# Moving two expert loads, seven weighted sums and two split positions in a Mamba and mixture-of-experts kernel

## The chip, the cores and the metric

The kernel runs on one core of one Trainium2 chip. The metric is the device time of one execution in microseconds (us); lower is better. A core has a matrix engine (PE, with its weight loads listed as PEld), a vector engine (DVE), an activation engine (ACT), GpSimd (POOL) and a sync engine (SP), which here issues all the DMAs. Each engine works through its own list of instructions in order, and an instruction that has to wait holds up everything behind it on the same engine.

## The reference

The input is 4 sequences of 1024 tokens with 128 features. Three layers are added to it in turn: a mixture of 8 experts (half weight), a Mamba layer, and the same mixture of experts again.

```python
x = x + 0.5 * _L0_ffn_ref(_layernorm(x, axis=-1), ...)
x = x + _L0_attn_ref(_layernorm(x, axis=-1), ...)
x = x + 0.5 * _L0_ffn_ref(_layernorm(x, axis=-1), ...)
```

The mixture computes every expert for every token and adds them with a weight per token:

```python
router_probs = softmax(x @ w_router)
gate_weights = softmax(x @ w_gating / GATE_TEMP)
h = silu(x @ w_gate[e]) * (x @ w_up[e])        # 128 -> 512, for each of 8 experts
expert_out = h @ w_down[e]                     # 512 -> 128
cw = router_probs * gate_weights
cw = cw / (sum(cw) + 1e-09)
out = sum over e of expert_out[e] * cw[:, e]
```

The Mamba layer projects to 2 x 256 channels, applies a causal convolution of 4 taps and Silu, derives the step `dt` (softplus) and the vectors B and C, and runs the recurrence `h = exp(dt * A) * h + dt * x * B` over 16 states per channel. Its output `sum(h * C) + D * x` is gated with Silu(z) and projected back. Everything is float32.

## The kernel before

**Tiling.** The 4096 tokens are cut into 8 blocks of 512 (`TB`), and a block lies transposed, 128 features by 512 tokens. Each block passes the mixture twice, so there are 16 mixture passes `s`; `order` lists them as (layer, block), beginning (1,0), (1,1). A pass goes through 8 experts. The text calls `s * E + e` a *position*: positions 0 to 7 are the first pass, 8 to 15 the second. The 512 hidden units of an expert are 4 chunks of 128, which are handled as 2 chunk pairs.

**One chunk pair.** `gate_part` makes the gate products in PSUM (`pg`, through `half_products`, lines 641 to 643) and takes Silu of them on ACT (`h`, line 625). `up_part` makes the up products (`pu`, the same lines) and multiplies them into `h` on DVE (line 657). `down` accumulates the expert's output in `pd`. Gate and up products are made of three fast matmuls: activations and weights are split into a rounded high part and a low part (`xh`, `xl`, `wh`, `wl`). The weights of an expert are split once, by two DVE instructions (`split_expert`, lines 298 and 299), from a raw buffer `wraw` into which `load_expert` brings them. Experts 0, 3 and 6 share one such buffer (tag `xc`), the others have two (tag `y`). `load_expert` issues three DMAs: gate and up weights to `wraw`, down weights to `wd`.

**Split positions.** For the positions in `SPL` the down product is made of three fast matmuls as well. That needs a split of the down weights (`wds`: ACT line 610, DVE line 612) and, for each chunk pair, `hh` on ACT (line 665) and `hl` on DVE (line 667); PE then runs the matmuls of lines 697 and 705, half an expert later than the ones it replaces. At other positions PE runs the plain float32 product of line 722.

**The weighted sum.** When an expert's `pd` is complete, ACT copies it to SBUF (`take`, line 735). Then `weight` multiplies it by the mixing weight `cwb` (line 744) and, except for the first expert, adds it to `acc` (line 747). Where `own` is true these are DVE instructions, else POOL's, in `pool_put`. `own` holds for positions 0 to 8 (`OWN = 9`) and for the whole last pass.

**The mixing weights.** `cwt` (line 556) transposes a pass's mixing weights, ACT copies them to `ct`, four small DMAs store them in DRAM (line 563), and `load_cw` reads them back spread over the 128 partitions (`cwb`, three buffers, line 588). In the first pass `cwt` stands at slot 11 (`CWT0`).

**Order.** All instructions are written out in an order that Python decides while it builds the kernel. Time is counted in *slots*, four for a chunk pair, 8 for a position, 64 for a pass. Each chain of events has slots at which its events are due; an event can also have a condition, and is forced when it is a number of slots late. `Plan` holds an estimated clock for each engine and puts the waiting pieces of DVE work (`put`, `fill`) and ACT work (`act_put`, `act_fill`) where they fit. `plan.need` writes out DVE work until a condition holds. Nothing in the order depends on times on the chip. Expert `e` is loaded at slot `8 * (e - 1) + WL`, with `WL = -5`, and its split is put at `8 * (e - 1) + WS`, `WS = 1`:

```python
    for e in range(1, E):
        add(8 * (e - 1), [(WL, lambda e=e: load_expert(e)), (WS, lambda e=e: split_expert(e))])
```

The Mamba layer of the first block starts around slot 77. Its scan (DVE lines 1015, 1021, 1033; ACT exponentials line 1002) starts when its softplus is done and goes on, block after block, until near the end.

Of the kernel before, what the change touches and what calls it, by code (L numbers as in the profile page):

```python
# [37 lines left out]
POW = 4  # L38
WL = -5
WS = 1  # L40
SPL = (*range(1, 11), *range(113, 127))
OWN = 9
CWT0 = 11
FENDS = {0: 8, 1: 9, 9: 9, 15: 8}
# [9 lines left out]
class Plan:  # L54
# [69 lines left out]
    def put(self, fn, cost, ready=0.0, low=False):  # L124
        it = [fn, cost, max(ready, 0.0), False]
        (self.lo if low else self.hi).append(it)
        return it
# [45 lines left out]
def tile_macaron_mamba_moe(  # L173
# [23 lines left out]
    E, _, F = w_gate.shape  # L197
# [20 lines left out]
    plan = Plan()  # L218
# [4 lines left out]
    def misc(name):  # L223
        if plan.reader in plan.spare:
            plan.act_need(plan.reader)
        plan.need(lambda: plan.reader is None or plan.reader[3])
        plan.wait_bank(name)
        return ps.tile([P, TB], F32, tag="misc", bufs=1, name=name)

    assert NBLK == 8  # L230
    order = [(1, 0), (1, 1), (1, 2), (1, 3), (2, 0), (1, 4), (2, 1), (1, 5), (2, 2), (1, 6), (1, 7)]
# [20 lines left out]
    def load_router():  # L252
        nc.sync.dma_start(out=wrg[:, 0:E], in_=w_router)
        nc.sync.dma_start(out=wrg[:, E:NE2], in_=w_gating)
# [19 lines left out]
    wh, wl, wd, raws, cast = {}, {}, {}, {}, {}  # L274

    def load_expert(e):
        tag, bufs = (("xc", 1), ("y", 2))[e % 3 > 0]
        raw = sb.tile([P, 2, F], F32, tag=tag, bufs=bufs, name=f"wraw_{e}")
        nc.sync.dma_start(out=raw[:, 0, :], in_=w_gate[e])
        nc.sync.dma_start(out=raw[:, 1, :], in_=w_up[e])  # L280
        if e == 0:
            load_router()
        wd[e] = const.tile([P, FC * H], F32, name=f"wd_{e}")
        nc.sync.dma_start(
            out=wd[e].rearrange("p (c h) -> p c h", c=FC),
            in_=w_down[e].rearrange("(c p) h -> p c h", p=P),
        )
        wh[e] = const.tile([P, 2, F], F32R, name=f"wh_{e}")
        wl[e] = const.tile([P, 2, F], F32R, name=f"wl_{e}")
        raws[e] = raw  # L290
# [5 lines left out]
    def split_expert(e):  # L296
        raw = raws.pop(e)
        plan.put(lambda: V.tensor_copy(wh[e], raw), 0.69, plan.pe)  # L298
        cast[e] = plan.put(lambda: V.tensor_tensor(wl[e], raw, wh[e].bitcast(F32), ALU.subtract), 1.21, plan.pe)  # L299
# [284 lines left out]
    def load_cw(s, e):  # L584
        d = ffn[s]
        kind, k = order[s]
        t = sb.tile([P, TB], F32, tag="cwb", bufs=3, name=f"cwb_{kind}_{k}_{e}")
        nc.sync.dma_start(out=t, in_=d["cd"][e, :].partition_broadcast(P))
        d["cwb", e] = t
        d["cwb_at", e] = max(plan.pe, d["cd_at"]) + 2.6  # L590

    def split(s, e):
        return s * E + e in SPL

    def gate_part(s, c):
# [7 lines left out]
        nm = f"{kind}_{k}_{c}"  # L603
        if f == 2 and s * E + e + 1 in SPL:
            x = (e + 1) % E
# [70 lines left out]
    def down(s, c):  # L676
        d = ffn[s]
        kind, k = order[s]
        e, f = divmod(c, FC)
        if f == 0:  # L680
            for o in list(ffn.values()):
                if "take" in o:
                    plan.act_need(o["take"])
            d["pd"] = ps.tile([P, TB], F32, tag="pd", bufs=1, name=f"pd_{kind}_{k}_{e}")
            if (s, e) == (len(order) - 1, E - 1):
                d["pds"] = d["pd"], misc("pd_end")
        h = d.pop(("h", c))
        cols = slice(f * H, (f + 1) * H)
        if len(h) == 2:
            ws = wds[s * E + e]  # L690
            w = ws["w"]
            if f % 2 == 0:
                plan.act_need(ws["wh"], d["hh", c])
                plan.need(lambda: ws["wl"][3])
                for q in range(2):
                    for i in range(2):
                        T.matmul(  # L697
                            d["pd"], w[:, i, (f + q) * H : (f + q + 1) * H], h[0][:, q, :],
                            start=(f + q + i == 0), stop=False,
                        )  # L700
                t = plan.on_pe(0.92, max(d["hh", c][4], ws["wl"][4]))
            else:
                plan.need(lambda: d["hl", c][3])
                for q in range(2):
                    T.matmul(  # L705
                        d["pd"], w[:, 0, (f + q - 1) * H : (f + q) * H], h[1][:, q, :],
                        start=False, stop=(f == FC - 1 and q == 1),
                    )
                t = plan.on_pe(0.46, d["hl", c][4])
        elif (s, e) == (len(order) - 1, E - 1):  # L710
            d["rest"] = d.get("rest", ()) + h
            if f % 2:
                for q in range(2):
                    part = slice(q * TB // 2, (q + 1) * TB // 2)
                    for g in (f - 1, f):
                        T.matmul(
                            d["pds"][q][:, 0 : TB // 2], wd[e][:, g * H : (g + 1) * H], d["rest"][g][:, part],
                            start=(g == 0), stop=(g == FC - 1),
                        )
            t = plan.on_pe(0.86, d["h_at", c])  # L720
        else:
            T.matmul(d["pd"], wd[e][:, cols], h[0], start=(f == 0), stop=(f == FC - 1))  # L722
            t = plan.on_pe(0.86, d["h_at", c])
        if f < FC - 1:
            return
        pd = d["pd"]
        edge = (s, e) == (len(order) - 1, E - 1)
        own = s * E + e < OWN or s == len(order) - 1

        def take():  # L730
            if e == 0:
                t = d["acc"] = sb.tile([P, TB], F32, tag="acc", bufs=2, name=f"acc_{kind}_{k}")
            else:
                t = sb.tile([P, TB], F32, tag="tmp", bufs=TMP, name=f"tmp_{kind}_{k}_{e}")
            S.copy(t, pd)

            def weight():
                cwb = d.pop(("cwb", e))
                at = max(plan.act, d["cwb_at", e])
                if e + 2 < E:  # L740
                    load_cw(s, e + 2)
                G_ = V if own else G
                put = (lambda f, cost, at: plan.put(f, 0.66, at)) if own else pool_put
                it = put(lambda: G_.tensor_tensor(t, t, cwb, ALU.mult), 1.25, at)  # L744
                if e > 0:
                    acc = d["acc"]
                    it = put(lambda: G_.tensor_tensor(acc, acc, t, ALU.add), 1.25, at)  # L747
                d["sum"] = it
                if e == E - 1:
                    d["tail"] = True  # L750
                    pool_run(None)

            if ("cwb", e) in d:
                weight()
            else:
                d.setdefault("late", []).append(weight)

        if edge:
            finish(d, d["pds"], k)
        else:  # L760
            d["take"] = plan.act_put(take, 0.58, t, True)
# [74 lines left out]
    def pool_run(after):  # L836
        credit[0] = min(credit[0] + CAP, CAP)
        while pend and (after is None or credit[0] > 0.0):
            pool_one(after)
# [309 lines left out]
    def add(base, evs, wait=WAIT):  # L1149
        chains.append([(max(0, base + ev[0]), wait, *ev[1:]) for ev in evs])  # L1150
# [13 lines left out]

    GPS = E
    add(0, [(0, lambda: load_expert(0))])
    for s in range(len(order)):
        add(8 * GPS * s, ffn_events(s))
# [8 lines left out]
        add(START[k], mid, 99)  # L1177
        add(START[k], back, 40)
    for e in range(1, E):
        add(8 * (e - 1), [(WL, lambda e=e: load_expert(e)), (WS, lambda e=e: split_expert(e))])  # L1180
    add(8 * E, [(-24, load_mamba)])

    S.preload_act_table_set("silu_and_others")
# [3 lines left out]
    with tc.manual_schedule(engines={ET.PE, ET.Activation, ET.DVE, ET.Pool, ET.SP}):  # L1187
        half = 0
        while chains or done < nst:
            c = 2 * half  # L1190
            todo = []
            while done < min(nst, c - 2 * (done // FC in SPL)):
                todo.append(done)
# [47 lines left out]
```

## Time and profile before

| | |
|---|---|
| time, 3 runs | 1262.14 us median (1262.1 to 1264.05) |
| the profiled execution | 1264.02 us, of which its span of instructions 1262.2 us |
| busy PE | 1245.7 us, 99% of the span |
| busy DVE | 1141.8 us, 90% |
| busy ACT | 920.8 us, 73% |
| busy POOL | 705.8 us, 56% |
| DMA | 115.09 MB, mean 91 GB/s |
| plain down product, line 722 | 824 instructions, two for each matmul call |
| Silu(g) * u, DVE line 657 | 256 instructions, 1214 ns |
| weighted sum on POOL, lines 744 and 747 | 98 pairs, 1348 and 1329 ns |

Busy time is the sum of the instructions' durations without overlaps; matmuls are pipelined, so a busy PE is not PE at its peak. The time around the span (1.8 us in the profiled execution) belongs to the launch and does not depend on the instructions. The span cut in 40 slices of 31.6 us, busy share in tenths (9 is 90% or more):

```profile
PE   9999999999999999999999999999999999999998
DVE  5986599999999999999999999999999999998676
ACT  6676887776778678877788787767876867656653
POOL 1012465767557656874576568656866575564400
PEclk9999999999999999999999999999999999999999
```

### The profile page before, as it was taken

Reading aid. Unit: us, or ns where it says so; the run is one execution under the profiler, and the core shown is the slowest. Engines: PE = TensorE matmul, PEld = TensorE weight load, DVE = VectorE, ACT = ScalarE, POOL = GpSimd, SP = SyncE. Lnnn points to the kernel's source line nnn. Section 1 sums busy time; section 2 is a strip of 40 time slices with the busy share of each in tenths; the row PEclk is TensorE's granted clock in tenths of the full one; section 3 lists DMA queues with packets and bytes.
Section 4 is the critical chain, followed back from the end, with each engine's and each line's share of the span. In section 5 each row is a group of like instructions: output and inputs, shape, how many; then the busy total and the mean of one; then the engine's idle time right before and its main releaser. Section 6 shows DMA issues by size and latency. Waiting matters only on the chain. (4 is left out here: it accounts for less than half of the span.)

```text
span 1262.2 us, 14418 instructions
## 1 busy us (share of the span) xinstructions
PE 1245.7 (99%) x4800; PEld 861.0 (68%) x4800; DVE 1141.8 (90%) x1286; ACT 920.8 (73%) x1324; POOL 705.8 (56%) x557
## 2 busy tenths in 40 slices
PE   9999999999999999999999999999999999999998
PEld 6777666666666666666666666666666666667887
DVE  5986599999999999999999999999999999998676
ACT  6676887776778678877788787767876867656653
POOL 1012465767557656874576568656866575564400
PEclk9999999999999999999999999999999999999999
DMA  4501333243333433333433343433433433311110
GB/s 135 171 24 36 103 109 90 88 127 86 96 95 92 120 89 95 96 102 104 99 97 99 92 113 95 113 84 86 109 96 90 110 97 112 100 60 40 29 42 25
DMA packets 75387, 115.09 MB, mean 91 GB/s; under 512 B 7473, under 2 KB 23729, under 8 KB 75313
## 3 DMA queue, kind: packets, MB, share of 16 engines
q1 hardware_dynamic: 75312, 114.19, 33.4%
q8 instruction: 37, 0.61, 0.2%
q14 instruction: 38, 0.30, 0.1%
HBM read 109.71 MB, written 4.46 MB: 90 GB/s over the span
## 5 line engine op out<-in xcount | busy, mean ns | idle before, releaser
L722 PE MATMUL pd<-h,wd 128*128 128x512 f32 x824 | 391.5, 592 | 0.0
L657 DVE TENSOR_TENSOR h<-h,pu 128x1024 f32<-128x1024 f32 x256 | 310.9, 1214 | 69.8 <-PE pu L643 44.2
L1036 POOL TENSOR_TENSOR y_m<-y_m,da_m 128x1024 f32<-128x1024 f32 x128 | 309.7, 2420 | 107.6 <-DVE hb_m L1015 97.0
L625 ACT ACTIVATE h<-pg 128x1024 f32<-128x1024 f32 x256 | 262.9, 1027 | 139.4 <-PE pg L643 134.0
L641 PE MATMUL pg<-xh_f,wh 128*128 128x512 f32 x510 | 263.1, 516 | 1.5 <-DVE wh L298 0.7
L744 POOL TENSOR_TENSOR tmp<-tmp,cwb 128x512 f32<-128x512 f32 x98 | 132.1, 1348 | 206.2 <-issue 79.3
L722 PEld LDWEIGHTS pd<-h,wd 128*128 128x128 f32 x824 | 153.8, 188 | 107.0 <-issue 89.9
L641 PE MATMUL pu<-xh_f,wh 128*128 128x512 f32 x512 | 204.5, 399 | 2.5 <-DVE h L657 2.2
L643 PE MATMUL pg<-xh_f,wl 128*128 128x512 f32 x510 | 201.1, 394 | 0.5 <-DVE wl L299 0.5
L643 PE MATMUL pu<-xh_f,wl 128*128 128x512 f32 x512 | 200.4, 391 | 0.0
L642 PE MATMUL pu<-xl_f,wh 128*128 128x512 f32 x512 | 199.9, 390 | 0.0
L642 PE MATMUL pg<-xl_f,wh 128*128 128x512 f32 x510 | 199.4, 391 | 0.0
L1015 DVE TENSOR_TENSOR hb_m<-dx_m,bcb_m 128x1024 f32<-128x1024 f32 x128 | 173.2, 1353 | 2.2
L1021 DVE TENSOR_TENSOR_SCAN hb_m<-da_m,st_sb,hb_m 128x512 f32<-128x512 f32 x128 | 164.3, 1283 | 2.4
L1002 ACT ACTIVATE da_m<-dt_m,A_sb 128x512 f32<-128x512 f32 x256 | 164.0, 711 | 0.6
L1021 DVE TENSOR_TENSOR_SCAN hb_m<-da_m,hb_m 128x512 f32<-128x512 f32 x128 | 156.5, 1223 | 2.6
L1033 DVE TENSOR_TENSOR da_m<-hb_m,bcb_m 128x1024 f32<-128x1024 f32 x128 | 155.8, 1217 | 2.1
L641 PEld LDWEIGHTS pg<-xh_f,wh 128*128 128x128 f32 x510 | 96.0, 188 | 66.2 <-issue 26.8
L747 POOL TENSOR_TENSOR acc<-acc,tmp 128x512 f32<-128x512 f32 x98 | 130.2, 1329 | 7.7
L642 PEld LDWEIGHTS pg<-xl_f,wh 128*128 128x128 f32 x510 | 96.3, 189 | 46.8 <-issue 32.5
L641 PEld LDWEIGHTS pu<-xh_f,wh 128*128 128x128 f32 x512 | 96.1, 188 | 31.2 <-DVE h L657 11.5
L643 PEld LDWEIGHTS pg<-xh_f,wl 128*128 128x128 f32 x510 | 95.6, 188 | 23.0 <-DVE wl L299 0.9
(181 smaller groups left out, 1488.8 us busy)
## 6 DMA issues: line engine op xcount, KB each, us to landing
bcb_m<-bc_m SPq DMA_DIRECT2D x128, 512.0 KB
cwb<-cd_f SPq DMA_DIRECT2D x128, 256.0 KB
out_dram<-x SPq DMA_DIRECT2D x13, 256.0 KB
x<-in_L_attn_x_dram SPq DMA_DIRECT2D x8, 256.0 KB
wraw<-in_L_ffn_w_gate_dram SPq DMA_DIRECT2D x8, 256.0 KB
wraw<-in_L_ffn_w_up_dram SPq DMA_DIRECT2D x8, 256.0 KB
wd<-in_L_ffn_w_down_dram SPq DMA_DIRECT2D x8, 256.0 KB
cd_f<-ct_f SPq DMA_DIRECT2D x64, 4.0 KB
```

The costliest lines, as they stand in the source:

```text
L625: S.activation(h, pg, AF.Silu)
L641: T.matmul(o[:, q, :], wh[e][:, i, cols[q]], d["xh"], start=True, stop=False)
L642: T.matmul(o[:, q, :], wh[e][:, i, cols[q]], d["xl"], start=False, stop=False)
L643: T.matmul(o[:, q, :], wl[e][:, i, cols[q]], d["xh"], start=False, stop=True)
L657: V.tensor_tensor(h, h, pu, ALU.mult)
L722: T.matmul(d["pd"], wd[e][:, cols], h[0], start=(f == 0), stop=(f == FC - 1))
L744: it = put(lambda: G_.tensor_tensor(t, t, cwb, ALU.mult), 1.25, at)
L1002: S.activation(da[:, i, :], d["dt"][:, i, :], AF.Exp, scale=A_sb[:, i, n : n + 1])
L1015: mul = V.tensor_tensor(hb, d["dx"], bcb[:, 0:1, :].to_broadcast([P, ND, TB]), ALU.mult)
L1021: V.tensor_tensor_scan(hb[:, i, :], da[:, i, :], hb[:, i, :], 0.0 if first else st_sb[:, i, n : n + 1], ALU.mult, ALU.add,)
L1033: V.tensor_tensor(da, hb, bcb[:, 1:2, :].to_broadcast([P, ND, TB]), ALU.mult)
L1036: it = pool_put(lambda: G.tensor_tensor(d["y"], d["y"], da, ALU.add), 2.4, plan.dve)
```

## The change

It has three parts.

1. *Loads.* A table `AHEAD` replaces `WL` for some experts. Expert 3 is loaded at slot 8 in place of 11, expert 4 at slot 10 in place of 19; both now come before the store of the mixing weights at slot 11. Experts 5 and 6 keep their slots. For experts from 4 on, `load_expert` first has the planner write out the split of expert `e - 3`.
2. *Sums.* `own` no longer holds for positions 0 to 6, so their seven products and six sums go to POOL. Positions 7 and 8 and the last pass stay with DVE.
3. *Split positions.* `SPL` begins with 1 to 12 in place of 1 to 10. Positions 11 and 12 are experts 3 and 4 of the second pass.

```diff
 WL = -5
 WS = 1
-SPL = (*range(1, 11), *range(113, 127))
+AHEAD = {3: -8, 4: -14, 5: -5, 6: -5}
+SPL = (*range(1, 13), *range(113, 127))
 OWN = 9
...
     def load_expert(e):
         tag, bufs = (("xc", 1), ("y", 2))[e % 3 > 0]
+        if e > 3:
+            plan.need(lambda: cast[e - 3] and cast[e - 3][3])
         raw = sb.tile([P, 2, F], F32, tag=tag, bufs=bufs, name=f"wraw_{e}")
...
-        own = s * E + e < OWN or s == len(order) - 1
+        own = (OWN - 3 < s * E + e < OWN) or s == len(order) - 1
...
     for e in range(1, E):
-        add(8 * (e - 1), [(WL, lambda e=e: load_expert(e)), (WS, lambda e=e: split_expert(e))])
+        add(8 * (e - 1), [(AHEAD.get(e, WL), lambda e=e: load_expert(e)), (WS, lambda e=e: split_expert(e))])
```

## The prediction

> **What bounds the kernel now.** I read the busy time by stage first, then PE's waits in the first 135 us, then the order of time of DVE, SP and ACT around each of those waits, last the chain of waits. Columns of the first: stretch, length, busy us (instructions) of PE, weight loads, DVE, ACT, POOL, clock, DMA share, GB/s.
>
> ```profile
> 28.00:36.00 8.00, 5.70 (x24) 4.05 (x23) 5.61 (x6) 2.80 (x4) 0.00 (x0) 1.00 0.98 316
> 36.00:70.00 34.00, 34.00 (x154) 27.86 (x153) 33.44 (x40) 23.57 (x30) 0.00 (x0) 1.00 0.43 121
> 70.00:82.00 12.00, 9.21 (x38) 6.71 (x37) 9.54 (x14) 9.44 (x21) 1.96 (x4) 1.00 0.00 0
> 107.00:140.00 33.00, 32.74 (x131) 22.74 (x130) 15.37 (x19) 19.21 (x27) 8.45 (x8) 1.00 0.27 78
> 170.00:1110.00 940.00, 937.46 (x3498) 624.51 (x3497) 895.91 (x988) 714.56 (x1024) 618.96 (x466) 1.00 0.38 100
> ```
>
> PE is the bound nearly everywhere: 937.46 of 940 us in the long middle, at a granted clock of 1.00. It has holes in two early stretches, 28 to 36 and 70 to 82 us. Between them PE is full, but DVE is too: 33.44 of 34 us. In 107 to 140 us DVE has more than half its time free. PE's waits in 0 to 135 us (total, times, longest):
>
> ```profile
> PE pd L705 <- DVE hl L667: 3.5, 2, 1.9
> PE pg L641 <- DVE wh L298: 0.7, 1, 0.7
> PE pg L643 <- DVE wl L299: 0.5, 1, 0.5
> PE pu L641 <- DVE h L657: 0.4, 1, 0.4
> ```
>
> All are waits for DVE. DVE, SP and ACT in order of time show what DVE was late with (start, length, instruction, idle time before it and its releaser):
>
> ```profile
> 28.84 0.69 DVE L744 TENSOR_TENSOR acc<-acc,cwb 128x512 f32<-128x512 f32 x1 [2.39 <-DMA cwb<-cd_f]
> 29.45 1.21 DVE L657 TENSOR_TENSOR h<-h,pu 128x1024 f32<-128x1024 f32 x1
> 32.09 0.69 DVE L298 CAST wh<-wraw 128x1024 fp32r<-128x1024 f32 x1 [1.42 <-DMA wraw<-in_L_ffn_w_up_dram]
> 33.96 1.22 DVE L667 TENSOR_TENSOR hl<-h,hh 128x1024 fp32r<-128x1024 f32 x1
> ```
> ```profile
> 21.23 1.35 SPq L563 DMA_DIRECT2D cd_f<-ct_f  x4
> 25.38 0.83 SPq L588 DMA_DIRECT2D cwb<-cd_f  x2
> 26.72 0.44 SPq L280 DMA_DIRECT2D wraw<-in_L_ffn_w_up_dram  x1
> ```
> ```profile
> 32.74 0.62 ACT L610 CAST wds<-wd 128x512 fp32r<-128x512 f32 x1 [4.43 <-DMA wd<-in_L_ffn_w_down_dram]
> ```
>
> Expert 3's weights are issued on SP behind the store of the mixing weights, which has to wait until 21.23. So DVE stands still twice (2.39 us for cwb, 1.42 us for expert 3) with hl queued behind, and ACT stands 4.43 us for the same expert's wd with the next Silu behind. A chunk pair takes PE 4.08 us undisturbed (gate products begin at 53.91 and 57.99). The pair begun at 28.80 took until 35.80: 7.00, a loss of **2.92**. The pairs of 66.15 to 71.11 and 71.11 to 76.03 lost 0.88 + 0.84 = **1.72** (expert 7's casts, started only at 70.28). The pair of 76.03 to 82.00 lost **1.89**; there hl stands in DVE's order behind an L657 that waits 1.41 us for PE.
>
> **The change, part by part.**
>
> *Loads.* Six DMAs (gate, up, wd of experts 3 and 4) move ahead of four stores and three cwb loads on SP. Expert 3's buffer is free when L479 ends (9.48 + 0.69 = 10.17), expert 4's when expert 1's casts end (10.80 + 1.23 = 12.03), and SP has issued nothing between 7.15 and 21.23. Six issues of about 0.45 take it to about 14.8. The new SP wait for expert 1's casts therefore has only the store behind it, 21.23 − 14.8 = 6.4 us later; without that cover it would cost its own 1.9 us. The added planner condition on old casts asks for work already passed (12.03 against a slot at about 20 us): nothing, and for experts 5 to 7 the casts lie more than 10 us back. Expert 3 landed 5.4 us after its issue (26.72 to 32.09) in a stretch of 316 GB/s; even twice that after 12 us is before 28.6, where DVE could want it. This takes away the 1.42 and the 4.43.
>
> *Sums.* 13 DVE instructions (one product for position 0, product and sum for 1 to 6) of 0.69, in all 9.0 us, become 13 of 1.29 on POOL, which has nothing from 24 to 70 us. That takes away the 2.39 as well: POOL waits for cwb now, with nothing queued behind but its own sums. POOL's longest product in the trace was 2.26 and its longest sum at 1110 to 1200 us 2.23: 4.5 us against 8.16 per expert, so it doesn't fall behind. What it takes from DVE, b per instruction, must be bounded:
>
> ```profile
> 1181.18 1.30 POOL L744 TENSOR_TENSOR tmp<-tmp,cwb 128x512 f32<-128x512 f32 x1 [5.97 <-ACT tmp L735]
> 1182.55 1.32 POOL L747 TENSOR_TENSOR acc<-acc,tmp 128x512 f32<-128x512 f32 x1
> 1183.20 1.75 DVE L667 TENSOR_TENSOR hl<-h,hh 128x1024 fp32r<-128x1024 f32 x1
> ```
>
> There the same three instructions meet: hl starts while POOL's sum runs, ends 1.08 us after it and takes 1.75 instead of 1.22, so it was held 0.53. In the five pairs of that block from 1153 to 1192 I find 0.53, 0.25 (hl of 1172.58, 1.47), 0.18 (a wds of 0.86 for 0.68) and otherwise nothing: 0.96 for ten instructions, b = 0.1. DVE is less full there, so I take b = 0.2. The upper end is 1.29, a whole POOL instruction; the lower 0.
>
> [...]
>
> With b = 0.2, DVE gains before expert 7's casts: 0.69 + 4 x 1.38 = 6.2 of sums, less 9 x 0.2 = 1.8, plus 3.8 of waits: 8.2 us. PE now asks for these casts 2.92 earlier, at 67.3 instead of 70.23, and they ended at 72.1, so 4.8 would do: the 1.72 goes too. The 1.89 is a matter of order, not of load; I count 0 for it (bounds 0 and 1.89).
>
> *Two more split positions.* Chain of waits, the two kinds of down product of one chunk pair:
>
> ```profile
> 1019.02 1.72 PE pd L722 x4
> 1136.29 0.91 PE pd L697 x4
> 1137.20 0.45 PE pd L705 x2
> ```
>
> 1.72 − 1.36 = 0.36 per pair, four pairs: **1.44** off PE. Price: per position on ACT one wds 0.62 and two hh 1.05, on DVE 0.68 and two hl 1.22; for both positions 5.4 and 6.2 us. They fall in 107 to 140 us, where ACT has 13.8 and DVE 17.6 us free. If that cover were gone it would cost up to those 6.2. Against it: the last pair's hl and down product move half an expert later, to where ACT is full (28.24 of 30 us in 140 to 170).
>
> **Sum.** 2.92 + 1.72 + 1.44 = 6.1, less 0.9 for POOL's blocks that fall on an hl PE is waiting for (a third of 13 x 0.2): **5.2**. Nothing later is tied to a clock, only to the order, and PE fills the middle, so it carries to the end. The profiled execution took 1264.02 us (span 1262.2), 1.9 above the median 1262.14; its span would be 1257.0, and the median **1257.0**.
>
> **Rivals.** A difference under 0.2% (2.5 us) cannot be told from none.
>
> *DVE stays the bound and gives the gain back.* PE's early arrival is worth only what DVE's list gets shorter: 3.8 + 13 x (0.69 − b) + 1.44. For b = 1.0 that is 1.2: **1261**. For it: DVE at 98% in 36 to 70. Against: b = 0.1 measured.
>
> [...]
>
> *The order of later work turns out worse.* The planner's clocks change, and events with a condition fall on other slots. The first exponentials of the scan (143.82 on ACT) need a slot of their own, one in eight; the next follow at 152.79. If the split positions' work pushes them by one, the scan starts 9.0 us later, and with DVE at 895.91 of 940 it regains little: +9.0 − 5.2, **1266**. It decides if the dt projection slips by 8 slots. Against: DVE idles before that point.
>
> **How the numbers follow.** Forecast 0.64, gain given back 0.12, lock 0.10 (0.03 of it within 0.2%), order 0.14. So faster 0.64, within 0.2% 0.15, slower 0.21. The forecast's own range is 1253.5 (the 1.89 goes too, no blocks) to 1259.5 (only loads, the splits at nothing); with the first two rivals 1253 to 1265.
>
> **What would show it.** DVE without a wait on a DMA after 20 us; expert 3's DMAs before 16 us; no PE wait at 33; 13 sums on POOL before 85 us, hl stretched by 0.2 on the mean; casts of expert 7 done before 67.5; four more L697 groups at 112 to 135. Wrong, if PE has new holes from 36 to 70 beside stretched hl, or the first exponentials come more than 1 us later after the start of the 27th chunk pair's gate than now.

## The result, and the profile after

The changed kernel takes 1268.67 us (median of 4 executions, 1268.28 to 1268.98) against 1262.12 us (4 executions, 1261.87 to 1264.05) for the kernel before: a ratio of 1.0048, with a 95% interval from 1.0035 to 1.0061. It is slower by 6.6 us where the forecast was 5.1 us faster. The profiled execution took 1268.45 us, its span 1266.6. Line numbers in `kernel.py` are 3 higher than before (722 is now 725, 697 is 700, 705 is 708, 657 is 660, 667 is 670, 735 is 738, 744 and 747 are 747 and 750, 298 and 299 are 301 and 302).

Busy time by stage after, with the columns of the table shown of before (stretch, length, busy us and instructions of PE, weight loads, DVE, ACT, POOL, clock, DMA share, GB/s):

```profile
28.00:36.00 8.00, 8.00 (x37) 6.63 (x36) 7.99 (x8) 5.25 (x7) 1.91 (x2) 1.00 0.49 132
36.00:70.00 34.00, 30.86 (x137) 24.27 (x136) 30.92 (x31) 19.64 (x26) 12.68 (x8) 1.00 0.39 105
70.00:82.00 12.00, 11.81 (x51) 9.19 (x50) 8.39 (x10) 11.50 (x27) 7.28 (x9) 1.00 0.00 0
107.00:140.00 33.00, 28.35 (x122) 21.47 (x121) 19.43 (x22) 22.26 (x29) 8.64 (x7) 1.00 0.24 67
140.00:170.00 30.00, 26.95 (x92) 17.47 (x91) 20.54 (x23) 22.59 (x30) 14.45 (x15) 0.94 0.23 62
...
170.00:1110.00 940.00, 937.60 (x3501) 624.59 (x3500) 896.88 (x988) 714.86 (x1030) 617.88 (x464) 1.00 0.38 100
```

Both old holes are gone: 28 to 36 us is full (5.70 us before) and 70 to 82 nearly so (11.81, was 9.21). Three new ones have come. In 36 to 70 PE is busy for 30.86 us where it had been full, in 107 to 140 for 28.35 where it had 32.74, and in 140 to 170 for 26.95 with a granted clock of 0.94 on the mean, where before it had this:

```profile
140.00:170.00 30.00, 28.99 (x105) 19.01 (x104) 26.45 (x30) 28.24 (x42) 18.79 (x16) 1.00 0.23 70
```

From 170 on nothing has changed. PE's waits in the first 150 us (total, times, longest):

```profile
PE pd L725 <- ACT tmp L738: 3.0, 1, 3.0
PE pd L700 <- ACT tmp L738: 2.8, 2, 2.7
PE pu L644 <- DVE h L660: 2.1, 2, 1.5
PE dbl_m L957 <- DVE ex_f L509: 1.4, 1, 1.4
...
PE lt_f L488 <- DVE xl_f L474: 1.0, 1, 1.0
```

The two largest waits are for ACT, for which PE had waited 1.4 us in all in the same stretch before. To see where time is won and lost I followed one event through all runs: the start of Silu of each chunk pair on ACT (line 628; 256 of them), less its start in the profile of before. A negative number is a lead. The last column is the end of the span.

| kernel | pair 7 (42 us) | 13 (68 us) | 20 (101 us) | 23 (115 us) | 29 (150 us) | 255 | span |
|---|---|---|---|---|---|---|---|
| the change | −2.5 | +1.5 | −2.2 | −1.9 | +5.3 | +4.4 | 1266.6 |
| p1_loads | −3.3 | −3.3 | −3.3 | −3.3 | −3.3 | −2.9 | 1259.3 |
| p2_sums | +0.6 | +4.5 | +0.9 | +0.9 | +0.9 | +0.8 | 1263.0 |
| p3_splits | −0.6 | −0.6 | −0.6 | −0.3 | +7.6 | +6.6 | 1268.8 |
| p4_loads_sums | −1.4 | +2.6 | −1.1 | −1.1 | −1.1 | −1.5 | 1260.7 |
| p5_loads_splits | −1.6 | −1.6 | −1.6 | −1.3 | +5.9 | +5.2 | 1267.4 |
| p6_split11 | −2.5 | +1.5 | −2.1 | −1.8 | −1.7 | −1.9 | 1260.4 |
| p7_take_first | −2.5 | +1.5 | −2.2 | −1.9 | −1.9 | −2.3 | 1260.0 |
| p8_best | −3.1 | −3.1 | −3.0 | −2.7 | −2.8 | −3.2 | 1259.1 |
| q1_short_sums | −3.1 | −2.9 | −6.7 | −6.7 | −6.7 | −7.1 | 1255.1 |
| q2_cast7 | −3.2 | −3.2 | −2.9 | −2.5 | −2.6 | −2.9 | 1259.4 |
| q3_logits | −3.2 | −3.2 | −3.3 | −2.9 | −4.2 | −4.9 | 1257.3 |
| q4_both | −1.6 | −1.6 | −2.8 | −2.5 | −3.7 | −3.9 | 1258.3 |
| r1_beside | −2.6 | −1.7 | −4.9 | −1.3 | +0.3 | +0.5 | 1262.7 |
| r2_beside_best | −3.3 | −2.8 | −6.1 | −0.8 | +3.5 | +2.9 | 1265.1 |

The first row tells two losses apart. One lies between pairs 7 and 13 (4.0 us, mostly won back by pair 20, because before loses its 1.72 and 1.89 us there), the other, 7.2 us, between pairs 23 and 29. After pair 29, the rest of the span changes it by 0.9 us.

One event in the profile of before shifts the whole table. Its store of the mixing weights landed late: SP issued the store at 21.23 and the read behind it only at 25.38 (both rows stand in the prediction), 4.15 us later. In p1_loads these are 2.43 us apart:

```profile
20.89 1.35 SPq L566 DMA_DIRECT2D cd_f<-ct_f  x4
23.32 4.18 SPq L591 DMA_DIRECT2D cwb<-cd_f  x4
```

The distance is 4.1 to 4.6 us in before, p4_loads_sums, p5_loads_splits, q1_short_sums and r1_beside, and 2.3 to 2.5 in the eleven others, whether the loads were moved or not. With the old loads and DVE's own sums, pairs 4 to 7 take 16.08 us in before and 14.17 in p3_splits, whose store landed early. By this comparison, the only one there is, about 1.9 us of each lead over before belongs to that one execution of before, which also took 1.9 us more than the median. Columns from pair 7 on can be compared within a row, and rows whose stores landed alike with each other.

### The profile page after: what moved, and what is told of

It reads as the page before. It is cut to its first block, busy times and chain, and to the rows that moved or that the text cites. A ratio compares the mean times of both kernels' runs of the same rounds, so it can differ in the third digit from the quotient of the medians.

```text
span 1266.6 us, 14457 instructions
## 1 busy us (share of the span) xinstructions
PE 1245.7 (98%) x4808; PEld 863.0 (68%) x4808; DVE 1144.3 (90%) x1279; ACT 924.5 (73%) x1330; POOL 725.0 (57%) x570
## 5 line engine op out<-in xcount | busy, mean ns | idle before, releaser
L725 PE MATMUL pd<-h,wd 128*128 128x512 f32 x808 | 385.6, 594 | 3.0 <-ACT tmp L738 3.0
L747 POOL TENSOR_TENSOR tmp<-tmp,cwb 128x512 f32<-128x512 f32 x104 | 142.1, 1366 | 235.8 <-ACT tmp L738 89.5
L725 PEld LDWEIGHTS pd<-h,wd 128*128 128x128 f32 x808 | 151.0, 189 | 108.1 <-issue 87.9
L1036 DVE TENSOR_TENSOR da_m<-hb_m,bcb_m 128x1024 f32<-128x1024 f32 x128 | 155.9, 1218 | 2.1
L750 POOL TENSOR_TENSOR acc<-acc,tmp 128x512 f32<-128x512 f32 x104 | 139.4, 1341 | 8.1
L646 PEld LDWEIGHTS pu<-xh_f,wl 128*128 128x128 f32 x512 | 96.1, 188 | 22.0
```

Of the source, the lines that this page charges most:

```text
L646: T.matmul(o[:, q, :], wl[e][:, i, cols[q]], d["xh"], start=False, stop=True)
L1036: V.tensor_tensor(da, hb, bcb[:, 1:2, :].to_broadcast([P, ND, TB]), ALU.mult)
```

## The experiments

**The three parts, alone and in pairs.** Each of the first five kernels carries some hunks of the diff and leaves the others as they were before. Loads alone:

```diff
+AHEAD = {3: -8, 4: -14, 5: -5, 6: -5}
...
+        if e > 3:
+            plan.need(lambda: cast[e - 3] and cast[e - 3][3])
...
-        add(8 * (e - 1), [(WL, lambda e=e: load_expert(e)), (WS, lambda e=e: split_expert(e))])
+        add(8 * (e - 1), [(AHEAD.get(e, WL), lambda e=e: load_expert(e)), (WS, lambda e=e: split_expert(e))])
```

> Only the two loads moved. Theory (the loss of the changed kernel comes from the split positions, and the loads are worth what was predicted for them): the Silu of pair 6 comes 3.6 us earlier than before, as in the changed kernel; DVE still does its own sums and is full from 36 to 70 us, so 0 to 1.5 us of it are given back at expert 7's casts; in all 2 to 3.5 us faster, 1259 to 1260. Rival (DVE is the bound there and gives everything back): same, 1261.5 to 1262.5.

1261.23 us, ratio 0.9988 [0.9978, 0.9997], which is 1.5 us (0.4 to 2.8). In the profile the lead of 3.3 us stands from pair 7 to pair 29 and is 2.9 at the end, but about 1.9 of it is the late store of before. With stores that landed alike, pairs 4 to 7 go from 14.17 us (p3_splits) to 13.11 (p1_loads), and from 16.08 (before) to 14.39 (p5_loads_splits): the loads alone are worth 1.1 or 1.7 us. The casts of expert 7 and the late `hl` still hold PE up afterwards (1.6, 0.7 and 0.5 us): the later terms do not go with the loads.

Sums alone:

```diff
-        own = s * E + e < OWN or s == len(order) - 1
+        own = (OWN - 3 < s * E + e < OWN) or s == len(order) - 1
```

> Only the sums moved to GpSimd. Theory: the trace of the changed kernel shows DVE stretched by about 0.6 us per GpSimd instruction (casts of 1.78 for 0.69, a wl of 2.20 for 1.22), nearly what each saves (0.69), so DVE is relieved by only about 1 us over 13 instructions, plus its 2.39 us wait for cwb, but the wait for expert 3 stays: between 1 us faster and 2 us slower, 1261 to 1264. Rival (the sums relieve DVE as predicted, 6.4 us): the losses at expert 7's casts and at pair 15 go, 3 us faster, 1259.

1265.01 us, 1.0018 [1.0009, 1.0027], 2.3 us slower. PE is 4.5 us late at pair 13 and 0.9 at pair 20. Work moved off the full engine, and the full engine was slower with it gone.

Split positions alone:

```diff
-SPL = (*range(1, 11), *range(113, 127))
+SPL = (*range(1, 13), *range(113, 127))
```

> Only positions 11 and 12 split. Theory (their late down products wait for the copy of the accumulator, which stands in ACT's list behind softplus and the first exponentials): PE loses 6 to 8 us between pairs 24 and 29, as in the changed kernel, 1268 to 1270, with PE waits of about 2.7 and 3 us for ACT's copy. Rival (the loss needs the moved sums or loads as well): 1.4 us faster, 1260.7.

1269.83 us, 1.0056 [1.0041, 1.0072]. These alone cost as much as the whole change: all of it between pairs 23 and 29.

Loads and sums, without the new split positions:

> The changed kernel without the two split positions. Theory: the gain of 2.2 us that it has at pairs 16 to 22 is kept to the end, 1259.5 to 1260.5. Rival (something else in the changed kernel, the later order, loses the 7 us): 1266 or more.

1261.84 us, 0.9995 [0.9985, 1.0005], no gain that is clear of noise. The interval overlaps with that of the loads alone, and the two profiles differ in when the store landed, so these two runs do not show what the sums take back from the loads; the experiment with short sums below does.

Loads and split positions, without the sums:

> The changed kernel with the sums back on DVE. Theory: the stretch from 36 to 70 us has no hl or cast held by GpSimd, so it stands at pair 16 where the loads alone stand; the split positions then lose their 7 us: 1266 to 1269. Rival (the sums on GpSimd shift DVE's and ACT's order and cause the loss at pairs 24 to 29): faster than before, 1258 to 1260.

1269.4 us, 1.0054 [1.0038, 1.0071], so the loads do not help the splits either.

**Why the split positions cost 7 us.** Here is ACT in the changed kernel (start, length, instruction, idle time before it and its releaser):

```profile
133.25 1.03 ACT L628 ACTIVATE h<-pg 128x1024 f32<-128x1024 f32 x1 [0.23 <-PE pg L646]
134.30 1.28 ACT L989 ACT_TABLE_LOAD   x1
135.59 1.06 ACT L989 ACTIVATE dt_m<-dt_m 128x1024 f32<-128x1024 f32 x1
136.55 0.57 ACT L738 COPY tmp<-pd 128x512 f32<-128x512 f32 x1
...
140.22 1.03 ACT L628 ACTIVATE h<-pg 128x1024 f32<-128x1024 f32 x1 [1.80 <-PE pg L646]
141.27 1.28 ACT L521 ACT_TABLE_LOAD   x1
...
142.82 2.54 ACT L1005 ACTIVATE da_m<-dt_m,A_sb 128x512 f32<-128x512 f32 x4
145.27 0.56 ACT L738 COPY tmp<-pd 128x512 f32<-128x512 f32 x1
```

And PE in the same stretch:

```profile
131.18 0.62 PE L708 MATMUL pd<-hl,wds 128*128 128x512 f32 x2
...
137.17 1.20 PE L700 MATMUL pd<-hh,wds 128*128 128x512 f32 x4 [2.66 <-ACT tmp L738]
...
140.93 0.61 PE L708 MATMUL pd<-hl,wds 128*128 128x512 f32 x2
...
142.52 0.39 PE L646 MATMUL pu<-xh_f,wl 128*128 128x512 f32 x1
145.88 3.47 PE L725 MATMUL pd<-h,wd 128*128 128x512 f32 x4 [2.98 <-ACT tmp L738]
148.36 1.42 PE L644 MATMUL pg<-xh_f,wh 128*128 128x512 f32 x1
```

Position 11 is complete in `pd` at 131.8 (131.18 + 0.62). Its copy comes on ACT only at 136.55, because the softplus with its table load stands ahead of it in ACT's list. `pd` has one PSUM buffer (`bufs=1`), so position 12's first product waits 2.66 us for that copy. The same happens again: position 12 is complete at 141.5, its copy stands behind the first exponentials and runs at 145.27, and PE waits 2.98 us. ACT is not short of time (it idles 1.80 us before 140.22); it is the order of its list. In the kernel before, position 12 was complete half an expert earlier, at 139.1 (137.21 + 1.88). The softplus stood ahead of its copy there too, but had just ended, and the next position's product at 141.70 did not wait:

```profile
138.38 1.06 ACT L986 ACTIVATE dt_m<-dt_m 128x1024 f32<-128x1024 f32 x1
139.35 0.57 ACT L735 COPY tmp<-pd 128x512 f32<-128x512 f32 x1
```
```profile
137.21 1.88 PE L722 MATMUL pd<-h,wd 128*128 128x512 f32 x4
141.70 1.88 PE L722 MATMUL pd<-h,wd 128*128 128x512 f32 x4
```

There is a third part. After the second wait the four products at 145.88 take 3.47 us, and the gate product behind them 1.42:

```profile
140.00:145.00 5.00, 2.91 (x13) 2.06 (x11) 1.98 (x3) 4.75 (x8) 1.24 (x3) 1.00 0.36 107
145.00:150.00 5.00, 4.12 (x7) 2.02 (x8) 3.05 (x4) 2.12 (x3) 3.65 (x6) 0.66 0.23 52
```

The granted clock is 0.66 over 5 us, 5.00 × 0.34 = 1.7 us lost. The three make 2.66 + 2.98 + 1.7 = 7.3, beside 7.2 in the table between pairs 23 and 29; what else differs there about cancels.

The test takes the order away and keeps all else of the change. Until slot 112, a waiting copy of `pd` is written to ACT's list ahead of the softplus and of the exponentials, and a down product ahead of that slot's events:

```diff
+    def takes_first():
+        for o in list(ffn.values()):
+            if slot[0] < 112 and "take" in o:
+                plan.act_need(o["take"])
...
+            takes_first()
```

> The changed kernel with both positions split, but the copy of the accumulator put ahead of softplus and of the first exponentials in ACT's list. Theory: the waits of 2.66 and 2.98 us fall to under 0.7 each and the clock stays at 1.00, so 5 to 7 us come back, 1261.5 to 1263.5; what stays is the 2 us at pair 24 and 25 where PE waits for the dt projection. Rival (the price is the work of the split itself or the buffers): 1267 to 1269.

1262.82 us, 0.9999 [0.9989, 1.0008]; the span is 1260.0, 6.6 below that of the change. ACT's list in this kernel:

```profile
134.19 0.58 ACT L738 COPY tmp<-pd 128x512 f32<-128x512 f32 x1
134.79 1.28 ACT L995 ACT_TABLE_LOAD   x1
...
139.38 0.58 ACT L738 COPY tmp<-pd 128x512 f32<-128x512 f32 x1
139.98 1.28 ACT L521 ACT_TABLE_LOAD   x1
```

and PE behind the second copy:

```profile
140.44 1.88 PE L725 MATMUL pd<-h,wd 128*128 128x512 f32 x4
141.75 0.79 PE L644 MATMUL pg<-xh_f,wh 128*128 128x512 f32 x1
```

The copies now stand ahead of the table loads. PE's waits for them shrink to 0.3 us, and the same four products take 1.88 us instead of 3.47. The lead at pair 23 (1.9 us) is kept to pair 29.

The other way round it is by one position. With only position 11 added, the late copies need not meet the softplus and the exponentials:

```diff
+SPL = (*range(1, 12), *range(113, 127))
```

> The changed kernel with position 12 not split, only 11. Theory (a split position's down product ends half an expert later and so meets softplus at the one and the exponentials at the other): with 11 alone the accumulator is copied before softplus and exponentials need it, the two waits of 2.7 and 3 us and the drop of the granted clock go: 1259 to 1261. Rival (each split position costs its share of ACT and DVE time): half of the loss stays, 1264 to 1265.

1262.19 us, 0.9997 [0.9987, 1.0006], 1.2 us above the range; but no 7 us are lost between pairs 23 and 29, and PE's waits for the copy are 0.2 us in all. It is the second position, added to the first, that makes the conflict; 12 without 11 was not run.

**What remains of the splits' gain.** Loads, splits and the copies put first, without the sums:

> Loads and split positions with the copy put first, sums on DVE. Theory: the loads' gain (what p1_loads shows) and the copy's, less the wait at pair 24: 1259 to 1262. Rival (DVE's own sums fill its list and the gain of the loads is given back): 1263 or more.

1261.61 us, 0.9989 [0.998, 0.9999], a span of 1259.1 against 1259.3 for the loads alone: the splits still bring nothing. PE's waits in this kernel show what ate it:

```profile
PE dbl_m L962 <- DVE ex_f L509: 1.4, 1, 1.4
```

`dbl_m`, the Mamba layer's product for dt, B and C, waits for the PSUM buffer in which router logits of the third mixture pass lie until DVE has read them, and that read stands behind an `hl` that the split positions brought. The next kernel moves these logits' chain for that pass alone:

```diff
+WHEN = {2: (-58, -53, -37, -35, -26, -11, 4),
...
```

> As p8_best, with the second step of the router's logits of the third pass two slots later, so that it comes after the projection of dt, B and C in PE's list and not before it. Theory (PE's waits of 1.4 and 0.6 us come from the one PSUM bank that both use, which DVE reads behind an hl): both waits go and 1 to 2 us are gained against p8_best. Rival (the projection waits for the convolution anyway): same as p8_best.

1259.67 us, 0.9963 [0.995, 0.9976]. The 1.4 us wait is gone (the one of 0.6 us stays), and the lead grows from 2.9 at pair 23 to 4.2 at pair 29. This kernel beats both the kernel before and the changed one. Its span is 2.0 us below the loads alone, both with an early store. How much of that is the splits' 1.44 and how much the moved logits was not separated: the logits were not moved without the splits.

**What the sums cost.** Here is DVE in the changed kernel around the first pair of sums (start, length, instruction):

```profile
35.11 1.78 DVE L301 CAST wh<-wraw 128x1024 fp32r<-128x1024 f32 x1
36.81 1.21 DVE L660 TENSOR_TENSOR h<-h,pu 128x1024 f32<-128x1024 f32 x1
```

and POOL in the same kernel:

```profile
34.50 1.84 POOL L747 TENSOR_TENSOR tmp<-tmp,cwb 128x512 f32<-128x512 f32 x1 [6.09 <-ACT tmp L738]
36.42 1.63 POOL L750 TENSOR_TENSOR acc<-acc,tmp 128x512 f32<-128x512 f32 x1
```

A cast that takes 0.69 us undisturbed takes 1.78 while POOL's product runs, and POOL's product, 1.29 undisturbed, takes 1.84: each has waited for the other. From 24 to 72 us five DVE instructions are stretched: three casts (1.78, 1.79 and 1.78), a split of the Mamba weights (1.51 for 0.41) and a `wl` (2.20 for 1.22), 1.09 + 1.10 + 1.09 + 1.10 + 0.98 = 5.36 us over nine POOL instructions. All five have their operands in SBUF. No line 660, which has one operand in PSUM, is stretched in this stretch: its eleven take 1.21 to 1.22 us. In the whole profile 171 of the 256 overlap a POOL instruction by more than 0.3 us; they take 1.21 us on the mean and the other 85 take 1.22. Loads and sums without the splits (p4_loads_sums) show the same five and one more, because the late store brings POOL's first product beside an `hl`:

```profile
28.83 2.29 POOL L747 TENSOR_TENSOR acc<-acc,cwb 128x512 f32<-128x512 f32 x1 [4.96 <-ACT wds L613]
29.89 2.32 DVE L670 TENSOR_TENSOR hl<-h,hh 128x1024 fp32r<-128x1024 f32 x1
```

That makes 5.36 + 1.10 = 6.46 us there.

To separate the block from the move itself, the next kernel has loads and sums, but POOL's 13 instructions work on one column of 512. It leaves out the weighting of the other 511 columns at positions 0 to 6:

```diff
-                it = put(lambda: G_.tensor_tensor(t, t, cwb, ALU.mult), 1.25, at)
+                w = slice(0, 1) if s * E + e <= OWN - 3 else slice(0, TB)
+                it = put(lambda: G_.tensor_tensor(t[:, w], t[:, w], cwb[:, w], ALU.mult), 1.25, at)
```

> Loads and sums (as p4_loads_sums), but GpSimd's 13 instructions of positions 0 to 6 work on one column of 512, so that the first experts' outputs are weighted in one column only; every list of instructions is unchanged. Theory (GpSimd holds up DVE's casts and splits for the length of its own instruction): the five casts and splits that took 1.5 to 2.2 us fall to their own 0.4 to 1.2, and the loss of 2 us against p1_loads goes: 2.5 to 4 us faster than before, about 1259. Rival (the changed order of DVE's list is what loses it): as p4_loads_sums, 1261.8, with the same waits of PE for h and xl.

1257.03 us, 0.9946 [0.993, 0.9963]. PE is full where it had holes, by the busy time of the stretch:

```profile
36.00:70.00 34.00, 34.00 (x154) 27.62 (x153) 28.38 (x32) 24.02 (x34) 4.67 (x7) 1.00 0.41 105
```

The same cast on DVE takes its 0.68 us:

```profile
35.13 0.68 DVE L301 CAST wh<-wraw 128x1024 fp32r<-128x1024 f32 x1
```

and POOL's product beside it 0.75:

```profile
34.51 0.75 POOL L748 TENSOR_TENSOR tmp<-tmp,cwb 128x1 f32<-128x1 f32 x1 [4.54 <-ACT tmp L738]
```

The lead grows to 6.7 us by pair 20, and no DVE instruction is stretched from 24 to 72 us. The spans of loads and sums with full and with one-column instructions, both with a late store, differ by 1260.7 − 1255.1 = 5.6 us. That is the price of the block on PE's path, most of the 6.46 us that DVE shows. In the changed kernel, with 5.36, the lead at pair 20 is 6.7 − 2.2 = 4.5 us short of this one.

Can the same 13 instructions be put where they do not block? This kernel starts each POOL instruction of positions 0 to 6 together with a line 660:

```diff
+            before = Last.ins
             V.tensor_tensor(h, h, pu, ALU.mult)
+            if pend and pend[0][6]:
+                pool_one(before)
```

> Loads and sums (as p4_loads_sums), with each GpSimd instruction of positions 0 to 6 tied to the DVE instruction just ahead of an L657 (h * pu), so that it starts beside the L657. Theory (a DVE instruction with one operand in PSUM is not held up by GpSimd; only those with all operands in SBUF are, so it is the place of GpSimd's instructions that costs, not their number): DVE's stretched instructions fall from 6.5 us in all to under 2, and 3 to 5.5 us of what q1_short_sums showed is reached: 1258 to 1260.5. Rival (GpSimd's instruction outlasts the L657 and holds the next one anyway, or comes so late that others wait for it): as p4_loads_sums, 1261.5 to 1263.

1264.6 us, 1.0013 [1.0004, 1.0023], above both ranges. Up to pair 20 it does what it should: DVE's instructions are stretched by 2.2 us in all (6.46 in p4_loads_sums), 1.1 of it again the first `hl`, casts take 0.73 us on the mean (1.34 there), `h` times `pu` still takes 1.22 on the mean, with POOL's instructions beside it at 1.28 to 1.30, and the lead is 4.9 us. Then it loses 5.2 us by pair 29, where PE waits for pieces of the Mamba layer (1.6 us for `xn_m` on ACT, 1.4 for an `xl` on DVE, 0.9 for ACT). Together with the copies first and the moved logits it behaves alike:

> The same tie, on top of q3_logits (loads, split positions with the copy first, logits later). Theory: the two gains lie in different stretches and add: 3 us better than q3_logits, ratio to before 0.993 to 0.995. Rival: the sums beside L657 shift the order at pairs 14 to 24 and cost as much as they bring, ratio 0.996 to 0.998.

1266.85 us, 1.0031 [1.0018, 1.0044], again outside both: a lead of 6.1 at pair 20, and 3.5 behind at pair 29. Part of this is the clock (0.66 over 105 to 110 us, 0.75 and 0.91 in 125 to 135: 3.4 us); the rest are waits for the Mamba layer's pieces. Holding POOL's sums back has changed the order of that layer's start, but which of its pieces comes late first was not separated; it stays open, and so does whether the block can be avoided at no cost.

**Order or capacity.** With loads alone, the casts of expert 7 still come late. If that is their place in DVE's list, putting them earlier takes the 1.72 away; if DVE is full, the wait only moves. The kernel is p8_best with one more edit:

```diff
-        add(8 * (e - 1), [(AHEAD.get(e, WL), lambda e=e: load_expert(e)), (WS, lambda e=e: split_expert(e))])
+        add(8 * (e - 1), [(AHEAD.get(e, WL), lambda e=e: load_expert(e)), (-3 if e == E - 1 else WS, lambda e=e: split_expert(e))])
```

> As p8_best, with expert 7's split put 4 slots earlier. Theory (the 1.2 us that PE waits for expert 7's casts, and hl's wait after it, come from the place of the casts in DVE's list, not from DVE being full, since with the loads alone all of DVE's work came 3.3 us earlier and the waits stayed): both waits of the stretch from 66 to 80 us go, 1 to 3 us faster than p8_best. Rival (DVE is full, an earlier cast only delays hl): no change against p8_best, waits moved to hl.

1261.36 us, 0.9986 [0.9975, 0.9997]. PE's waits for the casts are gone, and one wait of 2.27 us for `hl` stands in their place, in PE's order of time:

```profile
65.63 1.07 PE L700 MATMUL pd<-hh,wds 128*128 128x512 f32 x4
68.97 0.74 PE L708 MATMUL pd<-hl,wds 128*128 128x512 f32 x2 [2.27 <-DVE hl L670]
...
73.20 0.63 PE L645 MATMUL pu<-xl_f,wh 128*128 128x512 f32 x1
```

The busy time and the clock (0.66) of the stretch behind it:

```profile
70.00:75.00 5.00, 5.00 (x16) 3.97 (x15) 2.75 (x4) 1.98 (x3) 1.31 (x2) 0.66 0.00 0
```

So it is mostly capacity: the waits of 1.6, 0.7 and 0.5 us became one of 2.27. This profile also lost 5.00 × 0.34 = 1.7 us to the clock behind that wait. With the moved logits added:

> Both edits of q2_cast7 and q3_logits on p8_best. Theory: they lie 50 us apart and add, 3 to 5 us faster than p8_best, 1257 to 1259 where before is 1263. Rival: what is gained at 70 us is given back later, no better than the better of the two.

1260.2 us, 0.9969 [0.9956, 0.9982], which the intervals do not tell apart from q3_logits. Its profile shows a `hl` wait of the same 2.27 us with a clock of 1.00 after it, but a lower clock from 8 to 12 us (0.84 and 0.82 in 5 to 10 and 10 to 15), again 1.7 us.

## Why the prediction was wrong

**What bounds the kernel: right.** PE was held by DVE in the first 82 us, and PE filled the middle; every lead or lag of pair 60 is within 0.7 us of that at the end. (Not all of PE's waits were for DVE: one of 0.7 us for ACT's `xh_f`, at the start, was left out of the list. It is the same after.)

**Loads, 2.92: right about the event, mis-sized.** In the changed kernel expert 3's three DMAs were issued from 10.03 us on, and DVE has no wait on a DMA from 24 to 70 us. But the 2.92 was read from one execution, of 1264.02 us, in which the store landed late, and was taken off the median of 1262.14. Alone the loads gave 1.5 us by the ratio, and 1.1 or 1.7 from pair 4 to 7 where the stores landed alike. DVE's wait for `cwb`, 2.39 us in before, is 0.63 in p3_splits with the old loads and an early store, and with the new loads 0.35 in p1_loads (early) and 2.23 in p5_loads_splits (late): most of what the sums were to take away was the late store.

**Casts of expert 7, 1.72, and the 1.89: right about what they hang on, and mis-sized by the missing 1.89.** They do not go with the loads, as q2_cast7 shows for the casts; they go when DVE's list gets shorter, as I had argued for the 1.72. Together the terms are 2.92 + 1.72 + 1.89 = 6.53, and q1_short_sums, whose store landed as late as that of before, has 6.7 at pair 20. The 1.89, put down to order and counted as nothing, was a matter of load too.

**b = 0.2, and a third of it on PE's path, 0.9 us: wrong.** From 24 to 72 us DVE shows 5.36 us over nine POOL instructions in the changed kernel, 0.60 each, and 6.46 (0.72 each) in p4_loads_sums, of which 5.6 us reached PE instead of 0.9. I had b from a stretch at 1153 to 1192 us, where DVE is less full, and doubled it. In a stretch where DVE is busy for 33.44 of 34 us, a POOL instruction is much likelier to meet the one next in line, and what DVE loses there PE loses too. By the sum of the first rival, 3.8 + 13 x (0.69 − b) + 1.44, the whole gain is used up at b = 1.09; at 0.60 to 0.72 loads and sums together are level with before (0.9995). In the chances 0.10 goes to the upper end, b = 1.29 for every POOL instruction; no run shows it, and the runs showed 0.60 to 0.72 in its place. Three casts were stretched by 1.09 to 1.10 us beside POOL products of 1.84 to 1.86, which agrees with each waiting for the other, though not each POOL instruction found a DVE instruction to hold. I had the upper end in the text and gave the milder row the weight.

**Splits, 1.44 at no cost: the step that decided.** The 0.36 us per pair was right: in p7_take_first the split products begun at 137.72 make room for the next ones at 139.08, 1.36 us later, as reckoned. The price was wrong. I counted how many microseconds ACT and DVE had free in 107 to 140 us (13.8 and 17.6), and even named that "the last pair's hl and down product move half an expert later, to where ACT is full", and then put no price on it. The cover was counted in busy time. What mattered was the place of one 0.57 us copy in an in-order list, behind two table loads, a softplus and four exponentials, with the only buffer of `pd` hanging on it.

**The rivals.** None described it. "The order of later work turns out worse" had the right place and the wrong event: it asked whether the first exponentials come late. They came at 142.82 us, 1.0 earlier than before; the copy behind them was late. "DVE stays the bound and gives the gain back" is what happened to the sums, at b = 0.60 to 0.72 where it took 1.0.

**The signs named in advance.** The wait at 33 us is gone, the casts of expert 7 ended at 67.1, 13 sums ran on POOL before 85 us, and the new L700 groups are there. `hl` was not stretched from 24 to 72 us (1218 ns on the mean); the casts were. Two signs of being wrong came true. There are "new holes from 36 to 70", 34.00 − 30.86 = 3.1 us, though beside stretched casts and not beside stretched `hl`. And the first exponentials come 11.19 us after the gate products of the 27th chunk pair (131.63 to 142.82), where it was 9.77 (134.05 to 143.82): 1.4 us later, not because the dt projection slipped but because PE waited for the copy; with the copy first it is 9.89 (131.64 to 141.53). By the sum: the forecast span was 5.2 below 1262.2, the measured one is 4.4 above, 9.6 us apart. The splits make 1.44 + 6.3 = 7.7 of it (pair 23 to the end, −1.9 to +4.4); the other 1.8 is that the lead at pair 23 was 1.9 and not 2.92 + 1.72 − 0.9 = 3.74. Between the medians the miss is 1268.67 − 1257.0 = 11.7 us; the further 2 us are mostly that the late execution's losses were taken off the median. As an estimate, against a before whose store landed early the lead at pair 23 would be about nothing (1.9 − 1.9), which fits the 0.9995 of loads and sums. The low end of the range should have been 1254.2 by its own terms (1262.14 less 2.92 + 1.72 + 1.44 + 1.89 = 7.97), not 1253.5.

## What to carry to other kernels

Free time on an engine is no cover by itself: for an instruction that frees a single buffer, look at what stands ahead of it in its engine's list, table loads above all (1.28 us each here), and price the wait of the engine that needs the buffer next. Work moved off a full engine to one that can block it should be priced at the block it causes in that full stretch (0.60 to 0.72 us for each POOL instruction here), not in a slack one (0.1). A gain that is read off one profile should be read against where that execution lies among its kernel's times: here about 1.9 of 2.92 us were a store that landed late in it. And when a change has parts, each should be run alone: here one part alone gained 1.5 us, one cost 2.3 and one cost 7, by the ratios, and the first gain beyond the loads appeared only after two waits behind the splits had been taken away.

## What the runs showed of the hardware

Some waits of PE were followed by a lower clock and so cost more than themselves. In the profiles of the change and of q2_cast7 the granted clock was 0.66 over the 5 us that hold the work behind a wait (2.98 and 2.27 us), 1.7 us each. In the change it was 0.50 from 146.24 to 149.66, 3.42 us; in q2_cast7 PE's gate and up products started 0.43 us apart from 70.64 to 73.63, and 0.23 apart, each 0.39 to 0.40 long, before 70.26 and from 75.29 on. In p3_splits, around a wait of 2.66, it was 0.81 and 0.51 in two stretches of 5 us, 3.4 us, and in r2_beside_best it fell behind a wait of only 1.55 (0.66 over 105 to 110 us). But q4_both had the same 2.27 us wait with the clock at 1.00, and the 2.66 us wait of the changed kernel at 134.5 to 137.2 left it at 1.00 too, as did the one of 1.6 us for `xn_m` in r1_beside (1.00 in each 5 us from 85 to 110 us), so the length of the wait alone does not decide. What does was not shown.

POOL's instructions were themselves delayed beside a full DVE: in q1_short_sums a product on one column, 0.19 us at 69.91, took 0.75 at 34.51 beside DVE's work.
